# A graph layer's edge stages: VectorE and ScalarE take their work in source order instead of a scheduler's

## The chip, the cores and the metric

The kernel runs on one core of a Trainium2 chip. The metric is the device time of one execution in microseconds (us). A profiled execution gives the trace from which the details are read.

## The reference, cut to what matters

The input is 3125 nodes of 512 features and 53125 directed edges, sorted by target node. The kernel computes a layer norm, then two graph-attention layers, in parallel with them a linear-attention branch over the same nodes, and then a mixture of eight experts with the best two chosen. What the change touches is the graph attention, done twice (l = 0, 1), and the linear attention that is interleaved with it:

```python
q = ((x @ Wq[l].T + bq[l]) * scaling).reshape(n, H, DH)      # H = 8 heads, DH = 64
k = (x @ Wk[l].T).reshape(n, H, DH)
v = (x @ Wv[l].T).reshape(n, H, DH)
scores = jnp.einsum('ehd,ehd->eh', q[tgt], k[srcidx])
m = jax.ops.segment_max(scores, tgt, num_segments=n)
p = jnp.exp(scores - m[tgt])
s = jax.ops.segment_sum(p, tgt, num_segments=n)
w = p / (s[tgt] + 1e-16)
agg = jax.ops.segment_sum(w[:, :, None] * v[srcidx], tgt, num_segments=n)
x = _batchnorm(x + agg.reshape(n, D) @ Wo[l].T + bo[l], g1[l], beta1[l])
# ... feed-forward and a second batch norm

# linear attention: q, k = softmax over the 64 of each head, v plain
out = jnp.einsum('bhtd,bhde->bhte', q, context) * D_inv + q   # then @ Wp.T + bp
```

## The kernel before, in words

**Nodes and neighbours.** An earlier stage sorts the nodes by degree and puts them into 25 tiles of 128 (the last of 53). All nodes of a tile get as many neighbour slots as the tile's largest degree (CAPS: 44, 26, 23, ... 10); empty slots are masked. For each edge stage a DRAM table kvd holds a row of 1024 values, V then K, for each node.

**An edge stage** is one call of attention(l, ...) (L498). A tile is a Block of up to 26 neighbours (tile 0 is two Blocks of 22), and a Block goes in chunks of G = 2 neighbours: 26 Blocks and 232 chunks in a stage. For each chunk:

- two indirect gathers on GpSimd's queue (L583), of 128 rows of 4 KB each, into a place of one of the lanes (SBUF rings);
- a product of K with the tile's queries on VectorE (L588) and a sum over each head's 64 values (L589): the chunk's scores;
- once the Block has all its scores, on VectorE the mask (L598), maximum (L600), a floor under the maximum (L601) and its subtraction (L602), the exponential on ScalarE (L603), and on VectorE the sum (L611), an epsilon (L655), the reciprocal (L656) and the weights (L614);
- during the next Block's chunks V is weighed, chunk by chunk: three chunks of five on ScalarE, as 16 activations (L624), the others in one instruction on VectorE (L627);
- TensorE transposes the weighed rows and adds them up in PSUM (L644; L639 for the two Blocks of tile 0, which together(), L658, then merges).

**Lanes.** Stage 0 has five lanes of five places, stage 1 four of six (LANES, L47). Chunk n goes to lane n modulo the number of lanes. Two neighbouring places of a lane overlap by half: the K half of one is the V half of the next. So the gathers of chunk n can only start when the scores of chunk n-5 (stage 0) or n-4 (stage 1) have been taken, but for the first place of a lane's round, and when chunk n-20 has been added up.

**What runs beside it.** Each new tile needs its queries: in stage 0 places(t) gathers the node rows (part, L541) and transposes them, and query(t) multiplies (L555) and copies the result to q on ScalarE (L560). Each finished tile goes through finish(): a copy to aT (L688), the product with Wo (L701), the residual (L705) and statistics (L707). The generator beside() spreads the linear attention over the chunks: contexts(t) in stage 0, in five steps a tile, and mixed(t) in stage 1, in nine. Both start with a projection (L720, L723), take a softmax (maximum L731 on VectorE, exponentials L734 on ScalarE, reciprocal L740, product L773 and L775, or L814) and go on with TensorE; mixed(t) has also the division L829 and L830. A step's instructions are TensorE work and, right behind it in the source, the VectorE or ScalarE work that reads it.

**Who sets the order.** The kernel is written as one stream of instructions. A scheduler (Tile's) orders each engine's instructions by its own estimates of their durations, and puts in the semaphores that the data need. Nothing in the edge stages fixes an order in before.

**Ahead of stage 0.** bias_rows() splits a bias into three bfloat16 parts on VectorE (L514 to L518), which TensorE transposes (L521) and ScalarE copies (L522). One of the biases, mixb, is loaded by SP's queue once the branch that picks this path has been taken.

Of the kernel before, what the change touches and what calls it, by code (L numbers as in the profile page):

```python
# [12 lines left out]
OP = mybir.AluOpType  # L13
# [55 lines left out]

LAYER_COLS = 29  # L70
# [14 lines left out]
def gps_layer(ctx: ExitStack, tc: tile.TileContext, x, src, dst, cols, rows,  # L85
# [21 lines left out]
    kvd = [tc.dram_tile([N, 2 * D], F32, name=f"kvd{l}") for l in range(L)]  # L107
    wqo = [const.tile([128, NP, D], F32, name=name) for name in ("wq", "wo")]
# [280 lines left out]
    with tc.If(flag < 1) as fits:  # L389
        listed_layers(tc, cols=cols, rec=rec, idx=idx, mask=mask, kvd=kvd, zd=zd, ztd=ztd, xb=xb,  # L390
                      base=base, wqo=wqo, layer_weights=layer_weights, **args)
# [18 lines left out]
def listed_layers(ctx: ExitStack, tc: tile.TileContext, rows,  # L410
# [3 lines left out]
                  wqo, layer_weights):  # L414
# [10 lines left out]

    mixb = main.tile([128, L, NP], F32, name="mixb")
    for i, r in enumerate((ROW_BK, ROW_BQ)):
        nc.sync.dma_start(mixb[:, i, :], rows[r].rearrange("(c p) -> p c", p=128))
# [71 lines left out]
    def attention(l, stats, wq, wo, mixw):  # L500
        with tc.tile_pool(name="att", bufs=1, reuse_waits="tile") as ap, \
# [4 lines left out]
            taken_places = [0]  # L506

# [16 lines left out]

            c0 = l * LAYER_COLS + BQ
            bq = bias_rows("bq", colt[:, c0:c0 + NP])
            bm = bias_rows("bm", mixb[:, l, :])

            def places(t):

                n = TILES[t][1]
                gi = t // GT
                t0, k = FGROUPS[gi]
                if t == t0:
                    xg[gi] = main.tile([128, NP, GT * P], F32, name="xg", bufs=2)
                    if l:
                        w = min(N, (t0 + k) * P) - t0 * P
                        nc.sync.dma_start(xg[gi][:, :, :w], xin[gi, :, :, :w])
                if not l:
                    z = ap.tile([P, D], F32, name="part")  # L540
                    nc.gpsimd.indirect_dma_start(  # L541
                        out=z[:n], out_offset=None, in_=zd[:, :],
                        in_offset=bass.IndirectOffsetOnAxis(ap=node(t), axis=0))
                    o = (t - t0) * P
                    to_features(pp, "tr", xg[gi][:, :, o:o + n], z, n, nc.scalar.copy)
# [5 lines left out]
            def query(t):  # L551
                n = TILES[t][1]
                ps = pp.tile([P, 512], F32, name="pq", bufs=2)
                for c in range(NP):
                    nc.tensor.matmul(ps[:n], lhsT=of_place(t, c), rhs=wq[:, c, :],  # L555
                                     start=(c == 0), stop=False)
                nc.tensor.matmul(ps[:n], lhsT=one[:, :n], rhs=bq,
                                 start=False, stop=True)
                q = ap.tile([P, D], F32, name="q", bufs=2)
                nc.scalar.activation(q[:n], ps[:n], AF.Copy, scale=float(DH) ** -0.5)  # L560
                return q

            class Block:
# [9 lines left out]
                def scores(self, i):  # L573
# [7 lines left out]
                    for k in range(g):  # L581
# [6 lines left out]
                    nc.vector.tensor_mul(ks, ks, self.q[:n, None, :].to_broadcast([n, g, D]))  # L588
                    nc.vector.tensor_reduce(  # L589
                        self.sc[:n, :, j:j + g].rearrange("p h g -> p g h"),  # L590
                        ks.rearrange("p g (h d) -> p g h d", h=H), AX.X, OP.add)

                def exponentials(self):

                    n, w = self.n, self.w
                    sc = self.sc[:n, :, :w]
                    o = OFFS[self.t] + self.j0
                    nc.vector.tensor_add(sc, sc, mask[:n, None, o:o + w].to_broadcast([n, H, w]))  # L598
                    m = ap.tile([P, H], F32, name="m", bufs=3)
                    nc.vector.tensor_reduce(m[:n], sc, AX.X, OP.max)  # L600
                    nc.vector.tensor_scalar(m[:n], m[:n], FLOOR, None, op0=OP.max)  # L601
                    nc.vector.tensor_sub(sc, sc, m[:n, :, None].to_broadcast([n, H, w]))  # L602
                    nc.scalar.activation(sc, sc, AF.Exp)  # L603
                    self.m = m

                def weights(self):

                    n, w = self.n, self.w
                    sc = self.sc[:n, :, :w]
                    s = ap.tile([P, H], F32, name="s", bufs=3)  # L610
                    nc.vector.tensor_reduce(s[:n], sc, AX.X, OP.add)  # L611
                    if self.whole:
                        inverse_sum(s, n)
                        nc.vector.tensor_mul(sc, sc, s[:n, :, None].to_broadcast([n, H, w]))  # L614
                    self.s = s
# [33 lines left out]
            def scaled(o, agg, f, n):  # L649
                for h in range(H):  # L650
                    hs = slice(h * DH, (h + 1) * DH)
                    nc.scalar.activation(o[:n, hs], agg[:n, hs], AF.Copy, scale=f[:n, h:h + 1])

# [4 lines left out]
            def together(a, b, o):  # L658
# [13 lines left out]
                part = ap.tile([P, D], F32, name="part")  # L672
                for k, e, to in ((a, f[0], o), (b, f[1], part)):
                    nc.vector.tensor_mul(e[:n], e[:n], m[:n])
                    scaled(to, k.agg, e, n)
                nc.vector.tensor_add(o[:n], o[:n], part[:n])

            def finish(blocks):
# [10 lines left out]
                else:  # L689
                    a = ap.tile([P, D], F32, name="a")  # L690
                    together(blocks[0], blocks[1], a)
                    to_features(pp, "tr", at, a, n, nc.scalar.copy)
# [65 lines left out]
            def contexts(t):  # L758

                n = TILES[t][1]  # L760
                if t + 1 < FT:
                    turned(t + 1)
                z = zT.pop(t)
# [5 lines left out]
                ps = project(n, lambda c: z[:, c, :n], wv)  # L769
                yield  # L770
# [14 lines left out]
                elif t == FT // 2:  # L785
                    rowv.append(ap.tile([P, D], F32, name="a"))
# [14 lines left out]
            def mixed(t):  # L801

                n = TILES[t][1]
                if t + 1 < FT:
                    turned(t + 1)
                z = zT.pop(t)
                ps = project(n, lambda c: z[:, c, :n], wmq, bm)
                yield
                q = ap.tile([P, D], F32, name="mq")
                s = exponentials(q, ps, n)  # L810
# [4 lines left out]
                yield  # L815
                qT = ap.tile([128, NP, P], F32, name="mqT")
                to_features(pp, "tr", qT[:, :, :n], q, n, nc.scalar.copy)
# [17 lines left out]
                oT = ap.tile([128, NP, P], F32, name="mqT")  # L835
# [7 lines left out]
                nc.scalar.copy(oT[:, :, :n], ps[:, :NP * n].rearrange("p (c r) -> p c r", c=NP))  # L843
# [3 lines left out]
                y = ap.tile([P, D], F32, name="my")  # L847
# [4 lines left out]
            def beside():  # L852
                for t in range(FT):
                    yield from mixed(t) if l else contexts(t)
# [10 lines left out]
            each = 9 if l else 5  # L865
            steps, done, taken = beside(), 0, 0
            number = FT * each
            chunks = sum((w + G - 1) // G for t, j0, w in todo if t < FT - 2)
            chunks += (todo[0][2] + G - 1) // G

            before, held, ending = None, [], iter(())
            places(0)
            turned(0)
            q = query(0)
            places(1)
            for _ in range(each):
                next(steps)
                taken += 1
            for t, j0, w in todo + [(None, 0, 0)]:
                now, k = None, 0  # L880
                if t is not None:
                    now = Block(t, j0, w, q)
                    k = len(now.chunks)
                kb = len(before.chunks) if before else 0
                for i in range(max(k, kb)):
                    if i < k:
                        now.scores(i)
                        done += 1 if before else 2
                    if i == 0 and before:
                        before.weights()  # L890
                    if i < kb:
                        before.weigh(i)
                    next(ending, None)
                    while (taken - each) * chunks < (number - each) * done and taken < number:
                        next(steps)
                        taken += 1
                    if i < kb:
                        before.add_up(i)
                    if now and i == max(k - 4, 0) and j0 + w == CAPS[t] and t + 1 < FT:
                        q = query(t + 1)  # L900
                        if t + 2 < FT:
                            places(t + 2)
                for _ in ending:
                    pass
                if before:
                    held.append(before)
                    if sum(b.w for b in held) == CAPS[before.t]:
                        ending = finish(held)
                        held = []
                if now:  # L910
                    now.exponentials()
                before = now
            for _ in ending:
                pass
            assert next(steps, None) is None and taken == number
# [808 lines left out]
```

## Time and profile before

| | |
|---|---|
| three runs | 2830.23, 2837.37, 2837.75 us |
| median | 2837.37 us |
| profiled execution | 2804.75 us, its span 2803.0 us |
| TensorE's granted clock in it | 0.911 of full speed |
| busy over the span | PE 2398.1 us (86%), DVE 2054.1 (73%), ACT 1406.5 (50%), POOL 1414.4 (50%) |
| edge stage 0 | first gather 269.5 us, first product 284.1, end about 1085 |
| feed-forward, keys and values of layer 1 | 1085 to about 1347 us |
| edge stage 1 | first product 1347.2 us, end about 2245 |
| last feed-forward and experts | about 2245 to 2803 us |
| gathers of the edge stages (L583) | 906, mean 1267 ns on POOL, 6.3 us from issue to landing |
| products (L588) and scores (L589) | 464 each, mean 1193 and 1187 ns |
| weighing on VectorE (L627), on ScalarE (L624) | 214 of 1197 ns; 3888 that took 945.4 us |

PE is TensorE, DVE VectorE, ACT ScalarE, POOL GpSimd, SP SyncE; L588 is line 588 of the kernel. A row of a table of groups names line, engine, operation, the tile written and the tiles read, the shapes and the count; then busy us and the mean of one in ns; then the idle time of the engine just before these instructions, with what ended it. A row of the list of waits gives the waiting engine and line, what ended the wait, the us in total, the count and the longest. A row of a timeline gives the start in us, the length and the instruction, and in brackets the idle time ahead of it with what ended it.

### The profile page before, as it was taken

What the parts mean: (1) busy time and instruction counts of PE and PEld (TensorE: products, weight loads), DVE (VectorE), ACT (ScalarE), POOL (GpSimd) and SP (SyncE); (2) the same over time, 40 slices, a digit from 0 to 9 for tenths busy, and PEclk for the clock granted to TensorE, in tenths of its full rate; (3) what the DMA queues carried; (4) which work ended last, traced back from release to release, by engine and by line L of the source; (5) the groups of instructions that cost most, each with busy time, mean ns of one, the idle gap of its engine ahead of it and who ended that gap; (6) DMA issues with size and microseconds to landing.
All of it is one profiled execution on the core that took longest, in us unless ns stands there. A gap on an engine that the chain in (4) does not pass through costs nothing. (4 is left out here: it accounts for less than half of the span.)

```text
span 2803.0 us, 30800 instructions
## 1 busy us (share of the span) xinstructions
PE 2398.1 (86%) x8935; PEld 1302.4 (46%) x8935; DVE 2054.1 (73%) x3186; ACT 1406.5 (50%) x5315; POOL 1414.4 (50%) x1153
## 2 busy tenths in 40 slices
PE   6987989889889876999697787979888486999998
PEld 3442445545455543344344555555555344444443
DVE  7810999999999985500679888989988566666663
ACT  1111568787776763200276767776767423222220
POOL 3362778888777770011657766676765323222100
PEclk9998999999999987999798888989999796999999
DMA  8434999999999984321869888989887441111000
GB/s 287 171 121 138 328 331 337 332 330 338 330 326 325 332 266 159 122 108 78 286 234 335 287 299 292 329 303 331 309 307 269 131 135 51 34 48 48 32 19 20
DMA packets 214478, 620.58 MB, mean 221 GB/s; under 512 B 48068, under 2 KB 53569, under 8 KB 210199
## 3 DMA queue, kind: packets, MB, share of 16 engines
q0 software_dynamic: 161696, 518.18, 52.4%
q1 hardware_dynamic: 50048, 95.36, 9.4%
q10 hardware_dynamic: 2556, 4.97, 0.5%
q8 instruction: 75, 1.23, 0.2%
q14 instruction: 103, 0.84, 0.1%
HBM read 543.80 MB, written 74.75 MB: 221 GB/s over the span
## 5 line engine op out<-in xcount | busy, mean ns | idle before, releaser
L583 POOL DMA_INDIRECT lane<-kvd,idx x906 | 1147.7, 1267 | 526.7 <-issue 179.7
L624 ACT ACTIVATE lane<-lane,sc 128x64 f32<-128x64 f32 x3888 | 945.4, 339 | 117.9 <-DVE sc L614 117.6
L588 DVE TENSOR_TENSOR lane<-lane,q 128x1024 f32<-128x1024 f32 (+1 forms) x464 | 549.0, 1193 | 161.8 <-DMA lane<-kvd,idx 146.7
L644 PE MATMUL agg<-ident,lane 128*128 128x128 f32 (+1 forms) x3272 | 531.6, 301 | 140.5 <-DVE lane L627 59.5
L644 PEld LDWEIGHTS agg<-ident,lane 128*128 128x128 f32 (+1 forms) x3272 | 424.2, 154 | 316.1 <-ACT lane L624 143.5
L589 DVE TENSOR_REDUCE sc<-lane 128x16 f32<-128x1024 f32 (+1 forms) x464 | 545.5, 1187 | 2.6 <-ACT lane L624 1.6
L627 DVE TENSOR_TENSOR lane<-lane,sc 128x1024 f32<-128x1024 f32 (+1 forms) x214 | 252.3, 1197 | 0.1
L1089 DVE SCALAR_TENSOR_TENSOR yall<-py,prob,yall 128x512 f32<-128x512 f32 (+1 forms) x200 | 148.8, 748 | 112.4 <-PE py L1087 100.8
L555 PE MATMUL pq<-wq,xg 128*128 128x512 f32 (+1 forms) x400 | 201.7, 634 | 18.5 <-ACT kt L734 12.2
L701 PE MATMUL po<-aT,wo 128*128 128x512 f32 (+1 forms) x448 | 194.2, 572 | 20.3 <-ACT aT L688 13.4
L1087 PE MATMUL py<-w2t,hT 128*128 128x512 f32 (+1 forms) x400 | 188.7, 610 | 1.8 <-ACT hT L1083 0.8
L1080 PE MATMUL ph<-xT,w1t 128*128 128x512 f32 x320 | 156.3, 630 | 0.0
L1095 POOL DMA_INDIRECT out<-yall,rec x25 | 25.0, 1001 | 252.3 <-DVE yall L1089 247.4
L1083 ACT ACTIVATE hT<-ph,colt 128x512 f32<-128x512 f32 (+1 forms) x56 | 35.4, 633 | 211.0 <-PE ph L1080 210.8
L494 POOL DMA_INDIRECT kvd<-kv,rec x25 | 24.7, 989 | 222.8 <-DVE kv L491 216.8
L491 DVE COPY kv<-pv 128x512 f32<-128x512 f32 (+1 forms) x25 | 17.3, 692 | 153.4 <-PE pv L488 153.4
L701 PEld LDWEIGHTS po<-aT,wo 128*128 128x128 f32 x448 | 80.3, 202 | 97.9 <-issue 64.9
L1087 PEld LDWEIGHTS py<-w2t,hT 128*128 128x128 f32 (+1 forms) x400 | 71.9, 189 | 101.3 <-issue 69.0
L555 PEld LDWEIGHTS pq<-wq,xg 128*128 128x128 f32 (+1 forms) x400 | 73.4, 199 | 92.8 <-issue 68.3
L372 ACT COPY kv<-pkv 128x512 f32<-128x512 f32 (+1 forms) x50 | 29.2, 585 | 163.8 <-PE pkv L370 136.4
L1012 POOL DMA_INDIRECT bt<-base,rec x25 | 26.8, 1072 | 160.1 <-DVE yall L1019 150.3
L370 PE MATMUL pkv<-wk,xT 128*128 128x512 f32 (+1 forms) x200 | 100.7, 637 | 5.8 <-ACT kv L372 5.8
(264 smaller groups left out, 3288.4 us busy)
## 6 DMA issues: line engine op xcount, KB each, us to landing
lane<-kvd,idx POOLq DMA_INDIRECT x906, 6.3
kvd<-kv SPq DMA_DIRECT2D x24, 512.0 KB, 2.7
zT<-ztd SPq DMA_DIRECT2D x48, 256.0 KB, 5.3
xmid<-xg SPq DMA_DIRECT2D x10, 1024.0 KB, 5.7
xT<-xmid POOLq DMA_DIRECT2D x10, 1024.0 KB, 10.3
xr<-in_x SPq DMA_DIRECT2D x24, 256.0 KB, 3.9
xb<-xo SPq DMA_DIRECT2D x24, 256.0 KB, 5.6
zd<-z SPq DMA_DIRECT2D x24, 256.0 KB, 2.7
```

What stands on the lines that cost most here:

```text
L370: nc.tensor.matmul(ps[:n], lhsT=xT[t][:, c, :n], rhs=wkv[name][:, c, :], start=(c == 0), stop=(c == NP - 1))
L555: nc.tensor.matmul(ps[:n], lhsT=of_place(t, c), rhs=wq[:, c, :], start=(c == 0), stop=False)
L583: gets.append(nc.gpsimd.indirect_dma_start(out=kv[:n, k, :], out_offset=None, in_=kvd[l][:, :], in_offset=bass.IndirectOffsetOnAxis(ap=idx ...
L588: nc.vector.tensor_mul(ks, ks, self.q[:n, None, :].to_broadcast([n, g, D]))
L589: nc.vector.tensor_reduce(self.sc[:n, :, j:j + g].rearrange("p h g -> p g h"), ks.rearrange("p g (h d) -> p g h d", h=H), AX.X, OP.add)
L624: nc.scalar.activation(v[:, k, h, :], v[:, k, h, :], AF.Copy, scale=self.sc[:n, h, j + k:j + k + 1])
L627: nc.vector.tensor_mul(v, v, self.sc[:n, :, j:j + g].rearrange("p h g -> p g h")[:, :, :, None] .to_broadcast([n, g, H, DH]))
L644: nc.tensor.matmul(self.agg[:, c * n:(c + 1) * n], lhsT=kv[:n, k, c * 128:(c + 1) * 128], rhs=ident[:n, :n], is_transpose=True, start=firs ...
L701: nc.tensor.matmul(ps[:, :w], lhsT=wo[:, kk, c * 128:(c + 1) * 128], rhs=aT[gi][:, kk, :w], start=(kk == 0), stop=(kk == NP - 1))
L1080: nc.tensor.matmul(ph[:, :w], lhsT=w1t[:, e, c, :], rhs=xT[:, c, gs], start=(c == 0), stop=(c == NP - 1))
L1087: nc.tensor.matmul(py[:n], lhsT=hT[:, i * P:i * P + n], rhs=w2t[:, e, :], start=True, stop=True)
L1089: nc.vector.scalar_tensor_tensor(yall[:n, t, :], py[:n], prob[:n, i, e:e + 1], yall[:n, t, :], op0=OP.mult, op1=OP.add)
```

## The change

Inside attention() all work stands in a manual_schedule block for VectorE and ScalarE (ORDERED): these two take their instructions in the order of the source. TensorE, GpSimd and SP are still ordered by the scheduler. The source is rewritten for it:

- the scores of a chunk come after the product of the next chunk; only at a Block's end two scores follow each other;
- the mask is added at the end of a Block, maximum, subtraction and exponential come after the first product of the next Block, the sum after its second;
- the floor under the maximum is an operation of its own only for the two Blocks of tile 0; otherwise it is within the subtraction, now (max(m, floor) - score), with scale -1 in the exponential;
- adding up and the copies of q and of the transposed node rows are put on a list (later), which is run an iteration later;
- fetching, transposing and projecting the next tile's rows move to the iterations 2, 1 and max(k-4, 2) of a Block;
- mixed(t) is cut into more steps, two tiles of it are interleaved, and y goes through tile mo; mq gets two buffers; zT's load (SP queue) comes a step or two later in both generators;
- together() scales its second half and adds it in eight VectorE instructions, instead of eight ScalarE activations and one sum;
- mixb is loaded at the kernel's start, on ScalarE's queue.

The core of the diff:

```diff
+ORDERED = {mybir.EngineType.DVE, mybir.EngineType.Activation}
...
+    mixb = const.tile([128, L, NP], F32, name="mixb")
+    for i, r in enumerate((ROW_BK, ROW_BQ)):
+        nc.scalar.dma_start(mixb[:, i, :], rows[r].rearrange("(c p) -> p c", p=128))
...
-    mixb = main.tile([128, L, NP], F32, name="mixb")
-    for i, r in enumerate((ROW_BK, ROW_BQ)):
-        nc.sync.dma_start(mixb[:, i, :], rows[r].rearrange("(c p) -> p c", p=128))
...
+            def run_later():
+                now = later[:]
+                later.clear()
+                for do in now:
+                    do()
...
-                nc.scalar.activation(q[:n], ps[:n], AF.Copy, scale=float(DH) ** -0.5)
+                later.append(lambda: nc.scalar.activation(q[:n], ps[:n], AF.Copy,
+                                                          scale=float(DH) ** -0.5))
...
-                    nc.vector.tensor_scalar(m[:n], m[:n], FLOOR, None, op0=OP.max)
-                    nc.vector.tensor_sub(sc, sc, m[:n, :, None].to_broadcast([n, H, w]))
-                    nc.scalar.activation(sc, sc, AF.Exp)
+                    if not self.whole:
+                        nc.vector.tensor_scalar(m[:n], m[:n], FLOOR, None, op0=OP.max)
+                    nc.vector.scalar_tensor_tensor(sc, m[:n, :, None].to_broadcast([n, H, w]), FLOOR, sc,
+                                                   op0=OP.max, op1=OP.subtract)
+                    nc.scalar.activation(sc, sc, AF.Exp, scale=-1.0)
...
-                for k, e, to in ((a, f[0], o), (b, f[1], part)):
                     nc.vector.tensor_mul(e[:n], e[:n], m[:n])
-                    scaled(to, k.agg, e, n)
-                nc.vector.tensor_add(o[:n], o[:n], part[:n])
+                for h in range(H):
+                    hs = slice(h * DH, (h + 1) * DH)
+                    nc.vector.scalar_tensor_tensor(o[:n, hs], b.agg[:n, hs], f[1][:n, h:h + 1],
+                                                   o[:n, hs], op0=OP.mult, op1=OP.add)
...
             def beside():
-                for t in range(FT):
-                    yield from mixed(t) if l else contexts(t)
+                if l == 0:
+                    for t in range(FT):
+                        yield from contexts(t)
+                    return
+                ahead = iter(())
+                for t in range(FT + 1):
+                    now = mixed(t) if t < FT else iter(())
+                    for _ in range(6):
+                        next(ahead, None)
+                        next(now, None)
+                        yield
+                    ahead = now
...
-                for i in range(max(k, kb)):
-                    if i < k:
-                        now.scores(i)
-                        done += 1 if before else 2
-                    if i == 0 and before:
-                        before.weights()
-                    if i < kb:
-                        before.weigh(i)
-                    next(ending, None)
-                    while (taken - each) * chunks < (number - each) * done and taken < number:
-                        next(steps)
-                        taken += 1
-                    if i < kb:
-                        before.add_up(i)
...
+            with tc.manual_schedule(engines=ORDERED):
...
+                    for i in range(max(k, kb)):
+
+                        if i < k:
+                            now.products(i)
+                            done += 1 if before else 2
+                        if i == 0 and before:
+                            before.exponentials()
+                        if i == 1 and before:
+                            before.summed()
+                        if 0 < i < k:
+                            now.scores(i - 1)
+                        if i == 1 and before:
+                            before.weights()
+                            before.weigh(0)
+                        if 0 < i < kb:
+                            before.weigh(i)
+                        if i == k - 1:
+                            now.scores(i)
+                            now.masked()
+                        next(ending[0], None)
+                        run_later()
+                        while (taken - ahead) * chunks < (number - ahead) * done and taken < number:
+                            next(steps)
+                            taken += 1
+                        if i == 1 and before:
+                            later.append(lambda b=before: b.add_up(0))
+                        if 0 < i < kb:
+                            later.append(lambda b=before, i=i: b.add_up(i))
+                        if i == kb - 1:
+                            later.append(lambda b=before: summed(b))
+                        if now and j0 + w == CAPS[t]:
+                            if i == 1 and t + 1 < FT:
+                                turn_fetched(t + 1)
+                            if i == 2 and t + 2 < FT:
+                                fetch(t + 2)
+                            if i == max(k - 4, 2) and t + 1 < FT:
+                                q = query(t + 1)
+                    before = now
```

## The prediction

> **What bounds the kernel now.** I read the busy tenths first, to find the stages, then the table by windows for the two edge stages, then VectorE's groups and the list of waits in each, and last the timeline at the places where VectorE stands still. The edge stages run from 284 to 1085 us and from 1347 to 2245 us, 61% of the span; the change touches nothing else that costs time.
>
> In the table by windows (window, length, then busy us of PE, weight loads, DVE, ACT, POOL, granted clock, DMA share, GB/s) the first two rows are stage 0, the next two stage 1:
>
> ```profile
> 500.00:750.00 250.00, 219.98 (x932) 126.60 (x933) 234.21 (x292) 190.76 (x816) 201.02 (x156) 0.94 0.93 336
> 750.00:1000.00 250.00, 222.97 (x983) 131.74 (x981) 236.98 (x307) 190.38 (x806) 196.69 (x150) 0.95 0.91 322
> ...
> 1650.00:1900.00 250.00, 205.19 (x926) 132.90 (x924) 220.14 (x288) 185.70 (x777) 160.97 (x135) 0.88 0.88 313
> 1900.00:2150.00 250.00, 219.24 (x943) 134.83 (x944) 224.29 (x306) 179.56 (x746) 164.90 (x135) 0.92 0.87 314
> ```
>
> VectorE is 94% busy in stage 0 and 89% in stage 1; TensorE follows with 82 to 89%. So two things are open to the change: the idle 6% and 11%, and the length of VectorE's own work. DMA isn't the ceiling: from 278 to 286 us it moved 400 GB/s, against 336 at most here. VectorE's groups say what the idle time waits for (stage 0, then stage 1):
>
> ```profile
> L588 DVE TENSOR_TENSOR lane<-lane,q 128x1024 f32<-128x1024 f32 (+2 forms) x232 | 274.1, 1193 | 60.2 <-DMA lane<-kvd,idx 49.2 <-DMA part<-zd,rec 10.3 <-issue 0.5
> ```
> ```profile
> L588 DVE TENSOR_TENSOR lane<-lane,q 128x1024 f32<-128x1024 f32 (+2 forms) x232 | 274.8, 1193 | 101.6 <-DMA lane<-kvd,idx 97.5 <-ACT q L560 1.7 <-issue 1.2
> ...
> L731 DVE TENSOR_REDUCE hm<-pq 128x8 f32<-128x512 f32 (+1 forms) x25 | 17.0, 681 | 19.1 <-PE pq L723 19.0
> ...
> L829 DVE RECIPROCAL den<-mpo 128x4 f32<-128x4 f32 (+1 forms) x50 | 9.1, 181 | 9.3 <-PE mpo L821 9.3
> ```
>
> Most is waiting for gathers. Who holds those up in stage 1:
>
> ```profile
> POOL lane L583 <- issue: 101.0, 240, 6.3
> ...
> POOL lane L583 <- PE agg L644: 73.3, 64, 11.2
> ...
> POOL lane L583 <- DVE sc L589: 33.0, 38, 5.0
> ```
>
> "Issue" (0.3 to 0.4 us a gather) is POOL's own overhead; the others are a lane's place that is not free: gather n needs the scores of chunk n-4 (n-5 in stage 0) and the adding up of chunk n-20.
>
> **The change part by part.** The sum is made against the profiled run, 2804.75 us (span 2803.0), which lies 32.6 us, 1.2%, under the median of the runs.
>
> *Start of stage 0.* VectorE cuts the two biases by 273.60 and then waits 10.35 us for the first node rows, projected to queries in between:
>
> ```profile
> 273.60 0.16 DVE L518 TENSOR_TENSOR rest<-rest,cut 128x4 f32<-128x4 f32 x1
> 284.11 2.36 DVE L588 TENSOR_TENSOR lane<-lane,q 128x1024 f32<-128x1024 f32 x2 [10.35 <-DMA part<-zd,rec]
> ```
>
> After, mixb is loaded at the kernel's start instead of on SP's queue inside the branch, and the bias chain (5 us) with its transposes can lie before the first gather (269.52). Left are gather to landing (5.5 us), one transpose and projection: first product near 277, **-7** (bounds -9 and 0; if the chain waits as now, nothing). SP and ACT queues are idle enough there: one small load each.
>
> *Order of products and scores.* In before, the scheduler puts other work between an instruction and the one that needs its result: about 30 true dependent neighbours on VectorE in stage 0 and 53 in stage 1. Source order has 188 and 222: after each block mask after scores, subtraction after maximum, epsilon, reciprocal, weights and the first weighing in a row, and 25 to 50 pairs in the steps beside. The timeline shows both kinds (start, length):
>
> ```profile
> 1062.44 0.23 DVE L611 TENSOR_REDUCE s<-sc 128x8 f32<-128x88 f32 x1
> 1062.59 1.20 DVE L589 TENSOR_REDUCE sc<-lane 53x16 f32<-53x1024 f32 x1
> ...
> 1073.06 0.23 DVE L598 TENSOR_TENSOR sc<-sc,mask 53x80 f32<-53x80 f32 x1
> 1073.33 0.23 DVE L600 TENSOR_REDUCE m<-sc 53x8 f32<-53x80 f32 x1
> 1073.59 0.17 DVE L601 TENSOR_SCALAR m<-m 53x8 f32<-53x8 f32 x1
> ```
>
> Independent, the next starts 0.08 us before the first has ended; dependent, 0.04 us after (1073.06 + 0.23 to 1073.33). The difference is 0.12 us: 158 x 0.118 = 18.6 us in stage 0, 169 x 0.118 = 20 us in stage 1. The Trainium skill (VectorE: DVE Perf Modes, section The DRAIN you can't avoid) says that each operation drains in any case and a semaphore between two adds nothing; by it these 39 us are zero. The rows contradict it, so I take the rows. The dropped floor (0.17 us x 24, L601) gives back 2 us a stage with its gap; together() moves eight short operations from ACT to VectorE, +1 net.
>
> *What the order does to POOL.* A gather takes 0.94 us alone, 1.27 on average, because it stands still while VectorE's two-input operations run (L588, L627). The scheduler often puts two to four of these in a row; source order mostly one (194 single runs and 69 pairs, where before had 114, 75, 18 and 3). I estimate a quarter less blocking, 0.08 us x 453 = 36 us of POOL's time a stage. POOL in stage 0 is full (40 of 50 us busy, 31 gathers x 0.3 issue), so this is what its 34 us of waits for gathers after the start hang on. The Trainium skill (SBUF — State Buffer, section Who interferes with whom) would call these operations contenders only with a GpSimd instruction that reads SBUF, as a gather's index does; the row sets the size.
>
> *Interior of stage 0.* VectorE's work 711 + 18 - 1 = 728; idle 34 down to 10 or 25; now 756 in all: **-5**, bounds -18 and +8. Next late is VectorE itself.
>
> *Start of stage 1.* Before takes 101 us for the first 22 chunks (4.6 each; 3.5 later). The timeline shows why:
>
> ```profile
> 1433.22 0.16 DVE L668 TENSOR_TENSOR s<-s,fe 128x8 f32<-128x8 f32 x1
> 1443.37 0.69 DVE L731 TENSOR_REDUCE hm<-pq 128x8 f32<-128x512 f32 x1 [9.99 <-PE pq L723]
> 1446.60 0.20 DVE L740 RECIPROCAL hr<-hs 128x8 f32<-128x8 f32 x1 [2.54 <-ACT mq L734]
> ```
>
> There is no product from 1424 to 1448: the mixing steps were placed ahead of the next block and TensorE was late. Source order feeds the next products first: 22 x (4.6 - 3.6) = 22, less what one late step still costs: **-19** (bounds -24 and 0).
>
> *Interior of stage 1.* Here a score comes one product later than in 174 of 232 chunks before. From the end of score n-4 to the start of product n the trace shows 8.2 us (7.65 least: 0.7 to POOL, 2.6 two gathers, 4.5 to 5.5 landing). With the score right after its product a lane's loop is (8.2 + 2.3)/4 = 2.6 us a chunk, under VectorE's 3.27 (760/232). With product n+1 ahead of score n, four lanes give three chunks of run-ahead: (8.0 + 2.3)/3 = 3.4, and 3.7 with the mixing and normalizing steps in it; before ran at 720/205 = 3.51. Where a lane wraps (4 in 24) the wait is void. So 205 x 0.2 = 40, less the sixth that is void and less what faster gathers take off: **+25**, bounds 0 and +50. In stage 0 five lanes give 10.3/4 = 2.6, below the work.
>
> *Waits in a fixed order.* VectorE and ACT now stand at each step whose TensorE result is late, with all products queued behind (then lanes, POOL, gathers), and ACT's exponential behind the next product and 3.9 us of weighing (an ACT chunk is 16 x 0.243, from L624: 945.4/3888). The nearest rows are VectorE's own waits for PE in before (19.1, 9.3 and 4.7 in stage 1, 3 in stage 0), of which 26 remain without the start. The later list gives each result one iteration (3.3 us), but TensorE is 85% busy and its adding up is one iteration later too. Below: all 26 vanish; above: they come to 66. I take **+18**, nearer the row than either end. The double-buffered mq, the DMA of y from another tile and zT's transfer moved by a step or two (SP's queue holds little else) are at nothing: zT lands in 5.3 us, a step lasts 5; without that cover 25 x 2 us.
>
> Sum: -7 - 5 - 19 + 25 + 18 = **+12**, 2817 on the profiled run, 2849 on the median.
>
> **The rivals.** *Faster*: the lane loop stays hidden, since POOL is blocked less and 7.7 us suffices (10/3 = 3.3, what VectorE needs), and fixed waits are no more than before: -7 - 15 - 20 + 5 - 8 = -45, 2792. For it: 97.5 us of gather waits in stage 1, which a steady order could take. Against: 20 us of new gaps, and one chunk less run-ahead. It wins once the latency falls under about 7.7 us a loop. *Absorbed*: gaps fill waits that existed anyway and only the starts differ, or the scheduler's order on TensorE and POOL still sets the pace: 2837. *Much slower*: ACT and VectorE wait for each other at each of the 25 tiles of stage 1, 2 us each, on top of the sum: +60, 2897.
>
> **How the numbers follow.** Slower 0.48 (the sum, and with 0.1 the much slower), faster 0.33, absorbed 0.19. A difference under 0.3% (8.5 us) can't be told from no change. The likeliest is the sum, 2849, with its own range 2838 to 2880; the range for 8 in 10 takes in the faster case and most of the worst: 2790 to 2897.
>
> **What would show it.** First product near 277: start right. Dependent pairs 0.12 us apart from the others: gap right. POOL's gather mean near 1.19: blocking right. Stage 1 without a hole near 1440, its products every 3.6 us and POOL waiting more for scores than 33 us: loop right; at 3.3 the faster rival. VectorE's waits for PE at L767, L868 and L741 above 26 us in stage 1: fixed order right. Wrong it is if VectorE's idle share in stage 1 falls below 6%.

## The result: 3.4% slower

The changed kernel takes 2933.36 us (median of 4 runs, 2924.17 to 2934.8) against 2833.8 us of the kernel before in the same job (4 runs, 2828.76 to 2837.75): a ratio of 1.0343, 95% interval 1.0317 to 1.0368. In a second job, run as after_again below, it was 1.0296 (1.0234 to 1.0357). The prediction was 2849 us, +12, with a range up to 2897.

The jobs differ: the kernel before took 2834, 2800, 2850, 2850 and 2834 us (medians of five jobs), and the profile that the prediction was made from 2804.75 us. So kernels are compared by their ratio to the kernel before in the same job, and stages by two profiles from jobs in which before took 2850 us: before_third and after_again. Stage times are read from the trace, from the first product of a stage to its last scores:

| us | before_third | after_again | difference | predicted |
|---|---|---|---|---|
| span's start to first product | 306.6 | 299.1 | -7.5 | -7 |
| stage 0 | 790.2 | 837.0 | +46.8 | -5 |
| between the stages | 273.7 | 277.5 | +3.8 | 0 |
| stage 1 | 897.9 | 937.3 | +39.4 | -19 + 25 |
| after it | 571.5 | 572.5 | +1.0 | 0 |
| span | 2839.9 | 2923.3 | +83.4 | +12, with +18 for both stages' waits |

The table by windows of the changed kernel's first profile ("after"), in which stage 0 starts 13 us later than in the profile of before and stage 1 69 us (columns as before: PE, weight loads, DVE, ACT, POOL, clock, DMA share, GB/s):

```profile
500.00:750.00 250.00, 217.63 (x915) 131.41 (x915) 228.13 (x271) 188.28 (x799) 198.32 (x145) 0.90 0.90 314
750.00:1000.00 250.00, 206.92 (x899) 125.24 (x898) 224.09 (x274) 174.07 (x747) 191.17 (x145) 0.93 0.88 310
1700.00:1950.00 250.00, 204.67 (x842) 121.34 (x841) 208.45 (x257) 172.73 (x727) 150.30 (x119) 0.87 0.82 281
1950.00:2200.00 250.00, 211.16 (x908) 124.92 (x907) 216.06 (x281) 164.91 (x688) 153.01 (x123) 0.92 0.82 288
```

Every engine is less busy, VectorE 90 to 91% instead of 94 to 95% in stage 0, and DMA moves 310 to 314 GB/s there instead of 322 to 336. No engine has become a new bound; they wait for each other more. VectorE's groups, stage 0 and then stage 1 (line 613 is the product, 741 the residual, 869 the division in the mixing):

```profile
L613 DVE TENSOR_TENSOR lane<-lane,q 128x1024 f32<-128x1024 f32 (+2 forms) x232 | 277.0, 1194 | 87.4 <-DMA lane<-kvd,idx 83.9 <-PE agg L680 1.3 <-ACT lane L660 1.1
...
L741 DVE SCALAR_TENSOR_TENSOR xg<-po,colt,xg 128x512 f32<-128x512 f32 x20 | 15.0, 748 | 16.2 <-PE po L737 16.2
```
```profile
L613 DVE TENSOR_TENSOR lane<-lane,q 128x1024 f32<-128x1024 f32 (+2 forms) x232 | 277.2, 1195 | 128.6 <-DMA lane<-kvd,idx 120.1 <-PE agg L680 5.2 <-issue 2.5
...
L869 DVE TENSOR_TENSOR mo<-mpo,den 128x256 f32<-128x256 f32 (+1 forms) x50 | 21.2, 424 | 14.2 <-DMA base<-mo 12.0
```

Without the wait ahead of a stage's first product (22 us in stage 0), waits for gathers are 120 us in stage 1 (90.7 in the profile of before) and 62 in stage 0 (49.2). The wait for the product with Wo has grown, 16 us a stage against 0.8 and 4.7, and one for a store is new.

Summed over each stage in the pair of profiles, VectorE's time goes as follows. Stage 0: its own work and the gaps under 0.15 us +22.1, waits for gathers 26.5 to 53.0, for TensorE 6.5 to 22.5; waits for ACT and others 18 less. Stage 1: own work and gaps +21.0, gathers 82.3 to 114.4, the store +7.4, TensorE 39.6 to 21.1, the rest 3 less. VectorE's products in stage 0, before_third and then after_again:

```profile
L588 DVE TENSOR_TENSOR lane<-lane,q 128x1024 f32<-128x1024 f32 (+2 forms) x232 | 273.6, 1191 | 39.5 <-DMA lane<-kvd,idx 26.5 <-DMA part<-zd,rec 9.7 <-ACT lane L624 1.3
```
```profile
L613 DVE TENSOR_TENSOR lane<-lane,q 128x1024 f32<-128x1024 f32 (+2 forms) x232 | 277.0, 1194 | 82.1 <-DMA lane<-kvd,idx 53.0 <-ACT q L583 22.4 <-issue 3.1
```

The pair is not the whole record. In three profiles of before, stage 0's waits for gathers are 49.2, 37.3 and 26.5 us; in two of the changed kernel 61.8 and 53.0. All of VectorE's waits over 0.15 us together are steadier: 46 to 57 us in the three, 86 and 81 in the two. And of the 18 us that "others" lost, 10 are waits of the residual for which before_third's trace names no releaser.

### The profile page after: what moved, and what is told of

Read it like the earlier page. It is cut to its first block, busy times and chain, and to the rows that moved or that the text cites. A ratio compares the mean times of both kernels' runs of the same rounds, so it can differ in the third digit from the quotient of the medians.

```text
span 2932.8 us, 30740 instructions
## 1 busy us (share of the span) xinstructions
PE 2451.2 (84%) x8935; PEld 1318.8 (45%) x8935; DVE 2091.4 (71%) x3152; ACT 1396.6 (48%) x5299; POOL 1436.4 (49%) x1153
## 5 line engine op out<-in xcount | busy, mean ns | idle before, releaser
L608 POOL DMA_INDIRECT lane<-kvd,idx x906 | 1167.2, 1288 | 616.6 <-issue 242.3
L680 PE MATMUL agg<-ident,lane 128*128 128x128 f32 (+1 forms) x3272 | 584.3, 313 | 275.2 <-DVE lane L663 175.6
L680 PEld LDWEIGHTS agg<-ident,lane 128*128 128x128 f32 (+1 forms) x3272 | 444.6, 160 | 519.4 <-DVE lane L663 206.8
L756 PE MATMUL pq<-wmp,mqT 128*128 128x512 f32 (+1 forms) x200 | 118.2, 735 | 21.1 <-ACT mqT L883 20.8
L756 PE MATMUL pq<-wmk,zT 128*128 128x512 f32 (+1 forms) x200 | 109.2, 656 | 12.8 <-ACT kt L770 12.1
L638 ACT ACTIVATE sc<-sc 128x176 f32<-128x176 f32 (+14 forms) x52 | 16.8, 324 | 199.7 <-DVE sc L636 178.3
```

The source lines that it names most:

```text
L608: gets.append(nc.gpsimd.indirect_dma_start(out=kv[:n, k, :], out_offset=None, in_=kvd[l][:, :], in_offset=bass.IndirectOffsetOnAxis(ap=idx ...
L680: nc.tensor.matmul(self.agg[:, c * n:(c + 1) * n], lhsT=kv[:n, k, c * 128:(c + 1) * 128], rhs=ident[:n, :n], is_transpose=True, start=firs ...
L756: nc.tensor.matmul(ps[:n], lhsT=lhs(c), rhs=w[:, c, :], start=(c == 0), stop=(c == NP - 1 and bias is None))
```

## The experiments

**Is it the order, or the rewritten source?** First the kernel before again, and two that separate the change's halves. before_again is the kernel before unchanged.

> The kernel before, profiled once more, because its first profiled execution (2804.75 us) lay 29 us under the median of its runs (2834). What I expect: around 2834, with the 20 us stall of all engines near 198 to 221 us, which the profile of the changed kernel shows ahead of the edge stages, in this profile too; then it has nothing to do with the change. Rival: the stall belongs to the change (the earlier load of mixb); then this profile ends near 2805 again and has no such stall.

Measured: 2792.02 us, with no stall, in a job in which before took 2800. This spoke for the rival, but the changed kernel's profile came from a job in which before took 2834, so it told nothing; before_third, below, decides. free_order leaves the fixed order out:

```diff
-            with tc.manual_schedule(engines=ORDERED):
+            if True:
```

> The changed source, but without the fixed order: the scheduler orders VectorE and ScalarE again. If the fixed order is what costs (gaps between dependent neighbours, products ahead of scores, engines standing at late results): within 15 us of the kernel before, 2820 to 2850, with some 30 and 55 dependent neighbours again and gather waits in stage 1 near 98 us. If the new content costs (adding up and copies an iteration later, moved fetches, y in another step's tile): still above 2890.

Measured: 1.0033 (1.0019 to 1.0046), 2808.02 us against 2800.29. So nearly all of the loss is the fixed order; the rewritten source alone costs a third of a per cent. Its waits for gathers in stage 1 are 120 us all the same, not 98: the scheduler, given this source, puts scores ahead of the next product in only 80 of 231 chunks there (173 in before). before_fixed puts the old source's loop under the fixed order:

```diff
+            with tc.manual_schedule(engines=ORDERED):
                 before, held, ending = None, [], iter(())
                 places(0)
...
```

> The source before with the loop of the edge stages under the same fixed order for VectorE and ScalarE, nothing rewritten (the bias chain stays outside it). There each score follows its own product (232 more dependent pairs of 0.12 us a stage, 28 us) but comes ahead of the next product, and each step's VectorE work stands directly behind its TensorE work. If standing at late TensorE results is what costs most, this is the slowest of all, above 2990, with VectorE's waits for PE above 100 us a stage. If the lane loop (product ahead of score) is what costs most, it is faster than the changed kernel, below 2930, with POOL's waits for scores in stage 1 near 33 us or less.

Measured: 1.0412 (1.0388 to 1.0435), 2914.79 us. Neither number came: waits for TensorE are 11 us in stage 0 and 46 in stage 1, for ACT 15 and 60, but for gathers only 8 and 27. It is a test of the gap price: by the order of its instructions it has 428 dependent neighbours more than before in stage 0 and 449 in stage 1, and VectorE's work and gaps are 52.5 and 51.9 us more than in before_again, 0.12 us each. The prediction had 0.118. Here part of the gaps did fill waits for gathers, which fell by 29 us in stage 0 and 63 in stage 1; the stages grew by 40 and 59 us all the same. The other 23 us lie at the stages' starts (first product at 295.8 instead of 284.7 us, 286.6 instead of 275.1 us between the stages).

**The lane loop in stage 1.** five_lanes gives stage 1 the lanes of stage 0, and tile 0's merged rows another tile's memory to make room.

```diff
-LANES = ((5, 5), (4, 6))
+LANES = ((5, 5), (5, 5))
...
-                    a = ap.tile([P, D], F32, name="rowv")
+                    a = ap.tile([P, D], F32, name="mo" if l else "rowv")
```

> The changed kernel with five lanes of five places in stage 1 instead of four of six (tile 0's merged rows go to the mo tile to make room), so that gather n waits for the scores of chunk n-5. If the lane loop sets stage 1: VectorE's waits for gathers there fall from 120 to 80 us or less, POOL's waits for scores from 60 to under 20, and the time by 30 to 45 us, to 2890 to 2905. If the gathers wait for something else, or VectorE's own order sets the pace: under 10 us. Stage 0 unchanged in both.

Measured: 1.0173 (1.0146 to 1.0200), 2845.29 us, 1.2 to 1.7% below the changed kernel by the ratios, 35 to 48 us. VectorE's product group in its stage 1:

```profile
L613 DVE TENSOR_TENSOR lane<-lane,q 128x1024 f32<-128x1024 f32 (+2 forms) x232 | 276.7, 1193 | 51.1 <-DMA lane<-kvd,idx 41.2 <-ACT lane L660 5.1 <-ACT q L583 4.6
```

The waits for gathers fell from 120 to 41 us, with the same instructions in the same order on VectorE. The loop is shown. POOL's waits put down to scores did not fall (63 us): they aren't the measure of the loop that I took them for.

after_again is the changed kernel unchanged.

> The changed kernel once more, on the same chip as the runs beside it. Its first profile has a 16 us stall of all engines ahead of the edge stages (198 to 221 us) that the kernel with five lanes, the same code up to there, does not have. Expected: 3.3 to 3.6% above the kernel before, without the stall in the profile, edge stages near 836 and 940 us. If the stall belongs to the change it is there again.

Measured: 1.0296, 2932.77 us, and against the expectation the stall is there (first gather at 287.2 us). score_first undoes the order of product and score in both stages:

```diff
                             now.products(i)
                             done += 1 if before else 2
+                            if i < k - 1:
+                                now.scores(i)
...
-                        if 0 < i < k:
-                            now.scores(i - 1)
```

> The changed kernel with each chunk's scores directly behind its own product, still in fixed order. Undoes the lane loop in both stages, and makes 221 more dependent neighbours in each, 221 x 0.12 = 27 us. If the loop costs what five lanes showed (gather waits of 120 us in stage 1 down to 41): gather waits of stage 0 from 62 to under 30, of stage 1 to about 45, so -32 + 27 and -75 + 27: the kernel is 40 to 55 us faster than the changed one. If the loop binds only in stage 1 and stage 0 waits because GpSimd is full: stage 0 gets 20 us or more longer.

Measured: 1.0093 (1.0070 to 1.0115), 2876.4 us, 56 us under after_again. Stage 0 went from 837.0 to 819.6, stage 1 from 937.3 to 908.1, though VectorE's own work and gaps grew by 26 and 25 us: waits for gathers fell from 53.0 to 5.5 and from 114.4 to 27.3. So product-ahead costs stage 0 as well, where the prediction held five lanes for enough. VectorE's products in score_first, stage 0, and its wait for gathers in stage 1:

```profile
L613 DVE TENSOR_TENSOR lane<-lane,q 128x1024 f32<-128x1024 f32 (+2 forms) x232 | 276.6, 1192 | 28.0 <-issue 22.4 <-DMA lane<-kvd,idx 5.5
```
```profile
DVE lane L613 <- DMA lane<-kvd,idx: 27.3, 8, 9.6
```

The gathers, changed kernel (after_again) and then score_first, stage 0:

```profile
L608 POOL DMA_INDIRECT lane<-kvd,idx x445 | 584.9, 1314 | 189.8 <-issue 97.5 <-DVE sc L618 33.9 <-PE agg L680 19.0
```
```profile
L608 POOL DMA_INDIRECT lane<-kvd,idx x445 | 556.2, 1250 | 207.6 <-issue 99.2 <-PE agg L680 26.1 <-DVE sc L618 23.5
```

In before_third the mean is 1231 ns:

```profile
L583 POOL DMA_INDIRECT lane<-kvd,idx x444 | 546.8, 1231 | 182.7 <-issue 96.8 <-PE agg L644 27.6 <-PE tr L454 11.9
```

Over 0.945 us each, gathers stand still for 127 us in before_third's stage 0, 164 in after_again, 136 in score_first. Before_third is the lowest of three profiles of before (127, 146 and 154 us), so the pair overstates the rise. The two fixed orders are clearly apart: 156 to 177 us in the six profiles with products ahead of scores (after, after_again, five_lanes, and six_lanes, late_rows and order_pe below; means of 1297 to 1343 ns), 125 to 136 in the four with each score behind its own product (score_first, before_fixed, and fixed_best and score_five below; 1228 to 1250 ns). More gathers are held up, not each for longer: 228 of 445 take over 1 us in after_again, 186 in score_first. Runs of adjacent two-input operations did get shorter than in before (22 of three or four before, none after), and the blocking grew nevertheless; run length was the wrong measure. Why this order blocks more isn't settled.

six_lanes asks whether stage 0 waits by its lanes or by POOL:

```diff
-LANES = ((5, 5), (4, 6))
+LANES = ((6, 4), (5, 5))
```

> As five_lanes, and stage 0 with six lanes of four places instead of five of five (the same memory), so that there gather n waits for the scores of chunk n-6; in return it waits for the adding up of chunk n-18. If the lane loop is behind stage 0's gather waits too: they fall from 62 to 35 us or less and the stage from 836 to about 810. If GpSimd's own time (two gathers of 1.3 us and 0.3 us of issue each, 3.2 us a chunk) sets stage 0: no change beyond 8 us.

Measured: 1.0058 (1.0037 to 1.0079), 2864.91 us; stage 0 832.1 (after_again 837.0, five_lanes 835.9), waits for gathers 43.7 (53.0), those for TensorE 26.7 (22.5); stage 1, with five lanes, 881.8 against 937.3. A sixth lane does little for stage 0. POOL may hold it: in after_again POOL is busy for 616 us and, by an estimate from 0.3 us of issue a gather, another 143 of stage 0's 837, 91%. But the same sum gives 91% in before_third (576 and 143 of 790), so a full POOL alone doesn't tell the two kernels apart. That longer gathers on a full POOL hold stage 0 is likely, and not shown.

**Is before held by its four lanes too?** free_five is free_order with five lanes.

> The changed source without the fixed order (as free_order) and with five lanes in stage 1. free_order still waits 120 us for gathers in stage 1. If this is the lane loop: stage 1 from 896 to about 840, the kernel 1.5 to 2% below the kernel before. If the scheduler's order keeps them waiting: at most 10 us better than free_order.

Measured: 0.9889 (0.9862 to 0.9917), 2817.31 us: 1.1% faster than before, stage 1 858.2 us. before_five is the kernel before with five lanes (a and part of stage 1 share the tiles mo and my):

```diff
-LANES = ((5, 5), (4, 6))
+LANES = ((5, 5), (5, 5))
```

> The kernel before, scheduler's order, with five lanes of five places in stage 1 (tile 0's two temporary tiles share others to make room). Before waits 91 us for gathers in stage 1, but POOL waits there for scores only 33 us, and for the adding up 70. If the lane loop matters in before too: stage 1 from 882 to 858 or less, as with free_five, 1% below before. If four lanes are enough where scores come ahead of the next product: within 0.4% of before.

Measured: 0.9831 (0.978 to 0.9882), 2806.31 us against 2849.68; stage 1 861.1 us (897.9 in before_third), waits for gathers 38.8. This is the fastest version measured here. Lanes were scarce in before too, with POOL waiting only 33 us for scores.

**VectorE's waits for late results.** late_rows gives the residual another step and y its own tile:

```diff
                     yield
+                    yield
                     xs = xg[gi][:, c, :w]
...
-                y = ap.tile([P, D], F32, name="mo")
+                y = ap.tile([P, D], F32, name="my")
```

> The changed kernel with two waits of VectorE taken away by giving the result more time: the residual (L741) comes a step later behind its TensorE product, and y of the mixing has a tile of its own instead of mo's, so that VectorE's division doesn't wait for y's store. In the changed kernel these waits are 11 to 16 us for po in stage 0, 10 in stage 1, and 7 to 12 for the store in stage 1. If such stands in the fixed order cost what they show: 25 to 35 us less, about 1.1% . If the lane loop takes the time anyway (a stand of VectorE only moves what it would wait for gathers): under 12 us, with more waits for gathers instead.

Measured: 1.0303 (1.026 to 1.0346), no gain. The wait for the store is gone (7.4 to none in stage 1), and nothing came of it: the stage is 938.4 us, as 937.3. The wait for po rose, 10.7 to 20 us and 10.7 to 18.8. The trace shows why, in one place of late_rows. TensorE:

```profile
708.10 2.02 PE L680 MATMUL agg<-ident,lane 128*128 128x128 f32 x17
709.96 1.88 PE L757 MATMUL pq<-wmk,zT 128*128 128x512 f32 x4
711.68 3.60 PE L737 MATMUL po<-aT,wo 128*128 128x512 f32 x8
```

and VectorE (line 742 is the residual):

```profile
710.94 0.69 DVE L744 BATCH_NORM_STATS2 stats<-xg 128x6 f32<-128x512 f32 x1
715.99 0.75 DVE L742 SCALAR_TENSOR_TENSOR xg<-po,colt,xg 128x512 f32<-128x512 f32 x1 [4.36 <-PE po L737]
```

Two residuals stand side by side there: a Block has fewer iterations than finish() now has steps, and what is left over is flushed at the Block's end, each residual directly behind its own 3.6 us of TensorE. The kernel has made its point about the store, but isn't a clean test of the residual.

before_third is the kernel before once more, in a job in which it takes 2850 us.

> The kernel before, profiled on this chip. Expected: on a chip on which the kernel before takes about 2835 to 2850 us its profile has the first gather near 287 to 290 us, about 20 us later than in its first two profiles, as the changed kernel has there; then these 20 us are the chip's and not the change's. If its first gather is near 270 and its time above 2830, the extra time is elsewhere, and the delay of the first gather is the change's.

Measured: 2841.75 us, its first gather at 292.6 us. The kernel before has the stall too in such a job; it isn't the change's.

fixed_best puts scores first, five lanes and the later residual together:

> Fixed order with all that has helped: scores directly behind their product, five lanes in stage 1, the residual a step later. score_first stands 0.9% above before. If what is left there is VectorE's waits for PE (19 and 16 us) and for ACT (37 in stage 1): 15 to 30 us off, level with before. If the gaps between dependent neighbours (some 50 us in both stages) are the floor of a fixed order: still 0.5% or more above before, with under 10 us of gather waits a stage.

Measured: 1.0102 (1.0061 to 1.0142), 2876.13 us. Waits for gathers are 0 and 9 us; what is left is gaps (own work and gaps 781 us in stage 0, 734 in before_third), 12 and 45 us of waits for ACT and 23 and 23 for TensorE. score_five is the same without the residual's edit:

> The changed kernel with scores directly behind their product and five lanes in stage 1 (fixed_best without the later residual). If the lane loop is fully undone by either, the two don't add up: the kernel stands as score_first, 0.7 to 1.1% above before, and a fixed order's floor is its gaps and its waits for ACT and PE. If both are needed: 0.3% or less above before, with stage 1 below 880 us.

Measured: 1.0087 (1.0057 to 1.0116), 2856.72 us, as score_first: scores first and a fifth lane don't add up. They are two ways out of one loop. order_pe adds TensorE to the engines in source order:

```diff
-ORDERED = {mybir.EngineType.DVE, mybir.EngineType.Activation}
+ORDERED = {mybir.EngineType.DVE, mybir.EngineType.Activation, mybir.EngineType.PE}
```

> The changed kernel with TensorE in source order as well. In late_rows VectorE still waits 20 and 19 us for po, and TensorE is busy without a gap ahead of each of these waits, with other projections and adding up placed in front by the scheduler. If that placing is the cause: VectorE's waits for PE in the two stages (22 and 21 us in the changed kernel) fall to under 15 together, and the kernel is 10 to 25 us faster than the changed one, 2.1 to 2.6% above before. If it is TensorE's backlog, which source order has as well: waits and time as in the changed kernel, or worse since TensorE then stands too.

Measured: 1.0563 (1.0533 to 1.0593), 2991.62 us, VectorE's waits for TensorE 61 and 44 us. So the scheduler's order on TensorE isn't the fault: source order makes the waits longer. That they come from a backlog on TensorE fits this, and is not shown beyond the one place of late_rows above.

## Why the prediction was wrong

- **Start of stage 0**, -7: the number by luck, -7.5 in the pair. The bias chain does lie ahead of the first gather now (VectorE's part ends at 276.6 us in after_again, the gather starts at 287.2). But from first gather to first product it is 14.0 to 14.7 us in three profiles of before and 11.5 to 11.9 in two of the changed kernel: 2 to 3 us saved. The other 5 are a first gather at 287.2 instead of 292.6 us, after a shorter stall of the kind told of below; without that stall both kernels start it at 269 to 270 us (before_again, five_lanes).
- **Gaps between dependent neighbours**, 18.6 and 20 us: right in size, +22.1 and +21.0 with the other small changes of VectorE's work, and before_fixed gives 0.12 us a pair independently. The Trainium skill (VectorE: DVE Perf Modes, section The DRAIN you can't avoid), from which the prediction quoted that a semaphore costs nothing extra, also says there that a next operation that is not held starts earlier. That fits the independent pairs, which start 0.08 us before the end of the one ahead; it gives no size. The dependent ones show in the changed kernel as starts 0.03 to 0.04 us after that end:

```profile
1733.77 0.16 DVE L686 TENSOR_SCALAR s<-s 128x8 f32<-128x8 f32 x1
1733.96 0.20 DVE L687 RECIPROCAL s<-s 128x8 f32<-128x8 f32 x1
1734.20 0.33 DVE L651 TENSOR_TENSOR sc<-sc,s 128x160 f32<-128x160 f32 x1
1734.56 1.23 DVE L663 TENSOR_TENSOR lane<-lane,sc 128x1024 f32<-128x1024 f32 x1
```

- **The order and POOL**, "I estimate a quarter less blocking": wrong in sign. The gather's mean in stage 0 is 1343 and 1314 ns in the changed kernel, against 1292, 1274 and 1231 in three profiles of before, where 1190 was forecast.
- **Interior of stage 0**, "idle 34 down to 10 or 25 ... -5, bounds -18 and +8": this is the step that failed, 52 of the 71 us by which the sum missed (83.4 - 12). It let VectorE's idle time shrink by 9 to 24 us and so pay for the gaps. Instead its waits grew, from 46 to 57 us in all in the profiles of before to 81 and 86, and came on top of the 22 us of work and gaps. In the pair that is +26.5 for gathers, +16 for late TensorE results, which the sum had put mostly into stage 1, and -18 for others. score_first shows that product ahead of score makes the waits for gathers: without it 5.5 us of them are left. The sum's own figures don't close either: 711 of work and 34 of idle time are 745, not the 756 it starts from, so 11 us were left out.
- **Start of stage 1**, -19: half right. The hole near 1440 is gone, and the first 23 chunks take 91.9 us instead of 100.7: -9.
- **Interior of stage 1**, the lane loop, +25: right in mechanism, and near in size. Waits for gathers rose by 32 us in the pair. A fifth lane takes 55 us off the changed kernel's stage (937.3 to 881.8 in six_lanes) and 37 off that of before (897.9 to 861.1), so by single profiles the change added some 19 us to what four lanes cost.
- **The gaps of stage 1**: the prediction worked out 20 us of them and put them nowhere in the sum. They came, +21.0.
- **Waits in a fixed order**, +18: TensorE's waits +16 in stage 0, -18 in stage 1, the store +7. "At nothing" for y's tile was wrong by the 7 to 12 us that its wait shows; without it (late_rows) the time stayed. Stage 1 behind its first 23 chunks grew by 48 us where +25 and +18 were forecast; that this is near is luck, since the missing gaps and the waits that did not come nearly cancel.

The likeliest case named the right sign and two right mechanisms, the gaps and the lane loop, and came out at a seventh of the size since it let waits for gathers pay for the gaps, by a saving in POOL's blocking that no row had shown. No rival of the prediction reached +83 us.

## What to carry to other kernels

When an engine's idle time is waiting for transfers that this engine itself releases, don't count on it to absorb a gap or a later release: the idle time can grow with them, as it did here from 56 to 81 us in stage 0. Where each score followed its own product (before_fixed, score_first) waits for gathers did shrink while gaps grew. Count the run-ahead in buffers at each reordering (here one of four lanes), and try one more buffer before a new order; it was worth 1.7% where the new order lost 3.4%. A fixed order also puts dependent instructions side by side that a scheduler keeps apart, at 0.12 us a pair.

## What the runs showed of the hardware that was not expected

- In eleven of the sixteen profiles TensorE, VectorE and ScalarE stop two or three times ahead of the edge stages, between 193 and 223 us, in the kernel before as well. These are all the profiles from jobs in which before takes 2834 us or more; the four from the job at 2800 us and the prediction's profile of 2804.75 us don't have it. ScalarE in before_third:

```profile
206.29 0.58 ACT L357 COPY xT<-tr 128x512 f32<-128x512 f32 x1 [8.56 <-remote]
218.88 0.58 ACT L357 COPY xT<-tr 128x512 f32<-128x512 f32 x1 [12.00 <-remote]
```

"Remote" says that the trace has no releaser for it. The first gather comes some 23 us later in before_third than in before_again (292.6 and 270.0). The cause is open.
- With the same two-input operations in the same number, gathers stand still for 164 us of stage 0 when products run ahead of scores (after_again) and for 136 when each score follows its product (score_first). Without any overlap with such an operation a gather takes 0.98 us on average in after_again, with one 1.44.
